# A fixed order of products, sums and splits in the softmax attention of a hybrid block

## The chip, the cores and the metric

One core of a Trainium2 chip. The metric is device time of one execution in microseconds (us). The core has TensorE (PE, with a stream of its own for weight loads, PEld), VectorE (DVE), ScalarE (ACT), GpSimd (POOL) and SyncE (SP), which issues most DMAs. Each of these runs its own queue of instructions strictly in order; semaphores hold an instruction until what it needs on other engines is done. A scheduler arranges the program into these queues when the kernel is built.

## What is computed

Four residual blocks on x of shape (2, 1024, 512), all in fp32: a chunked linear attention, a gated FFN with quantized weights (called f), a softmax attention (b), and the same FFN again (g).

```
x = x + attn_a(layernorm(x))      # 4 heads of 128, chunks of 128 tokens, 2 x 8 chunks
x = x + ffn(layernorm(x))         # 512 -> 1408 -> 512
x = x + attn_b(layernorm(x))      # 512 wide, one head, 2 x 1024 tokens
x = x + ffn(layernorm(x))

# attn_a, per chunk
attn  = (q k^T) * beta * tril(exp(cla - cla^T))    # cla: cumulated log of alpha
y     = attn v + (q state) * exp(cla)
kw    = k * beta * exp(cla_end - cla)              # the weighted keys
state = state * exp(cla_end) + kw^T v

# attn_b
out = softmax(Q K^T / sqrt(512)) V W_o

# ffn
down(silu(gate(x)) * up(x)),  W = (wq - 128) * scale
```

## The kernel before

**Products.** Every large product is made of three: each operand is split into a high half (a copy in a reduced format, on ScalarE) and a low half (the rest, a subtraction on VectorE or GpSimd), and hi·hi, hi·lo and lo·hi are added up in PSUM (`split`, L83; `mm3`, L95). A product in this text is one TensorE instruction of 512 columns. There are 8 PSUM banks, and 12 shared buffers of 128 x 2048 fp32 ("slots"), given out in turn: a new slot waits until its last user has been read.

**Order.** The code emits steps, and the scheduler orders them on each engine by data and its own priorities. `behind(instructions)` (L76) sets an edge: what is emitted inside is put, on the same engine, after those instructions in the queue. It adds no wait on data. DMAs issued from SP and from POOL stand in these engines' queues with the rest.

**Stage A (L338 to L718)** runs over 16 tiles t of 128 tokens. For each: projections `pWk`, `pWv` (24 products, `kv_tile`), norms of the keys (`k_norm`, L543 on: square on ScalarE, sum and factors `s1`, `s2` on VectorE, a power and the weighted keys `kw` on GpSimd), the keys' transpose `pkT` and its copy `kT`, `pd` (kw^T v), the chunk's outputs `pl` and `pg`, and the scores `pS`. `decay(t)` (L494 on) masks `row` on GpSimd (L500) and makes the decays `dec` with four exponentials on ScalarE (L512). Between tiles, `fill[t]` holds steps that prepare later stages: norms of later rows, moves, and `a_split`, which splits the transposed input of later tiles (`xT_a`).

**Layer norms into transposed form** (`ln_norm`, `ln_move`, L175 to L210): a normalised tile is transposed in 32 x 32 blocks by VectorE into a buffer `y` (L195), of which there is one, and 16 DMAs a block of 512 tokens move the pieces to their places in `xT` (L205). A line in `ln_move` chooses the queue that issues them. `combine` (L223 on) then makes the operands of a seven-product scheme: B11, B21, B12, B22 and the sums T1 to T4, each split and in a slot of its own.

**FFN (L721 to L855)** makes two passes of 1024 tokens over 11 hidden blocks of 128. Per block: products P1, P6, P5, P7 into X, Y, Z, V, copies and sums on ScalarE and VectorE (`u2`, `up`), then P2, P3, P4, and the gated result split into `hs`, in part on GpSimd. Each pass ends with eight output tiles (`pof`, `pog`). During it, steps of what comes next are handed out: the argument `after` holds, for FFN f's second pass, norms and moves of attention b's first rows and the 12 steps of their `combine`.

**Attention b (L858 to L1123)** has two batches b of 1024 tokens. Weights are loaded by `blocks` (L860, DMAs L868): `wvo` for the values, `wm` for the queries, both into slots. `v_tile` makes eight value tiles (`pvb`, 12 products each), `q_proj` the queries (`pqb`). Then four cycles n, each for two tiles of 128 query rows: `scores_head` (P1, P6, P5, P7: 24 products into psX, psY, psZ, psV, then the copies and sums `u2b`, `upb`), a `between` (24 products: two query projections or an `out_b`), `scores_tail` (P2, P3, P4: 18 products, then the softmax of both tiles). The scores' left operands A11, S2, S1, S3 (for the head) and A12, A22, S4 (for the tail) come from `q_operands`, each with a cast on ScalarE and a subtraction on VectorE (`opA`, `opS`).

Probabilities go through DRAM: `probs_T` transposes 32 x 32 blocks on VectorE into `py`, writes them by one DMA (L996) and reads them back by four (L1004) into `ptl`, then splits them into `pth` and `ptl`. `out_b(b, i)` (`pob`, 24 products) takes these and the value tiles. `do(steps, n)` hands out n steps of norms, moves or `combine`, behind the last softmax.

Of the kernel before, what the change touches and what calls it, by code (L numbers as in the profile page):

```python
# [34 lines left out]
def hybrid_block_kernel(ctx: ExitStack, tc: tile.TileContext, a, out):  # L35
# [59 lines left out]
    def mm3(ps, lhs_hi, lhs_lo, rhs_hi, rhs_lo, first, last):  # L95
        nc.tensor.matmul(ps, lhs_hi, rhs_hi, start=first, stop=False)  # L96
        nc.tensor.matmul(ps, lhs_hi, rhs_lo, start=False, stop=False)  # L97
        return nc.tensor.matmul(ps, lhs_lo, rhs_hi, start=False, stop=last).ins  # L98

# [97 lines left out]
    def ln_move(nm, st, b):  # L197

        if b == 0:
            lnT[nm, st] = slot(f"xT_{nm}{st}").rearrange("p (k c) -> p k c", k=KD)  # L200
        y = lnY[nm, st]
        xf = lnT[nm, st].bitcast(F32).rearrange("p k (i b q) -> p (k i) b q", i=ST, b=4)
        queue = nc.gpsimd if (nm, st) in (("b", 2), ("b", 3), ("g", 0), ("g", 1)) else nc.sync
        for c in range(4):
            queue.dma_start(  # L205
                out=xf[32 * b : 32 * (b + 1), :, c, :],
                in_=y[32 * c : 32 * (c + 1), b].rearrange("p k i q -> p (k i) q"),
            )
# [129 lines left out]
    with ExitStack() as actx:  # L338
# [201 lines left out]
        def k_norm(t, after=None):  # L540
# [15 lines left out]
            if t % NC < NC - 1:  # L556
                s2 = mp.tile([P, H], F32, tag="s2", name=f"s2{t}")
                nc.vector.tensor_tensor(s2, s1, ec[:, 1, i, :], ALU.mult)
                kw = tl("kw", t)
                weighted = nc.gpsimd.tensor_tensor(kw, kf, s2.unsqueeze(2).to_broadcast([P, H, P]), ALU.mult)  # L560
                normed[t] += (weighted.ins,)
            kva[t] = kf, kw, v
# [118 lines left out]

        fill[3].insert(0, lambda: a_split(2))
        fill[7].insert(0, lambda: a_split(3))
        moving = combine("f", 0)
        wcs, loads = [], []
        for t in range(NT):
# [12 lines left out]
            if t + 1 < NT:  # L699
                decay(t + 1)  # L700
            with behind(normed.get(t + 1, (weighed,))):
# [19 lines left out]
    def ffn(src, dst, nm, wcs, moving, ended, after):  # L721
# [3 lines left out]
        with ExitStack() as fctx:  # L725
# [5 lines left out]
            for pr in range(2):  # L731
# [86 lines left out]
                for i in range(2 * ST):  # L818
# [25 lines left out]
                    if pr == 0 and i == 4:  # L844
                        wcs = [stationary(n, f"{nm}1") for n in range(2)]

    ffn(
        x1,
# [4 lines left out]
        spilled,  # L853
        (ln_steps(x2, "b", 0) + ln_steps(x2, "b", 1), combine("b", 0)),
    )  # L855
# [4 lines left out]
    with ExitStack() as bctx:  # L860
# [57 lines left out]
        def score_product(ps, b, n, nm, first):  # L918
            a_, x = {
                "P1": ("A11", "B11"), "P2": ("A12", "B21"), "P3": ("S4", "B22"), "P4": ("A22", "T4"),  # L920
                "P5": ("S1", "T1"), "P6": ("S2", "T2"), "P7": ("S3", "T3"),
            }[nm]
            o, w = QA[b, n, a_], XT["b", b, x]
            for k in range(2):
                for i, j in ((0, 0), (0, 1), (1, 0)):
                    nc.tensor.matmul(  # L926
                        ps,
                        o[:, i, k],
                        w[:, j, k],
                        start=first and k == 0 and i + j == 0,  # L930
                        stop=k == 1 and i == 1,
                        skip_group_check=nm != "P6",
                    )

        def scores_head(b, n):
# [6 lines left out]
            up = bp.tile([P, 512], F32, tag="up", name=f"upb{b}{n}")  # L942
            nc.scalar.copy(up, Z)
            nc.vector.tensor_tensor(Z, Z, u2, ALU.add)
            nc.vector.tensor_tensor(V, V, u2, ALU.add)
            nc.vector.tensor_tensor(up, V, up, ALU.add)
            heads[b, n] = X, Z, V, up
# [9 lines left out]
        def softmax(t, halves):  # L957
# [3 lines left out]
            nm = mp.tile([P, 1], F32, tag="nm", name=f"nm{t}")  # L961
            nc.vector.tensor_tensor(nm, mx[:, 0:1], mx[:, 1:2], ALU.max)
            nc.vector.tensor_scalar(nm, nm, -SC, None, ALU.mult)
            pe = bp.tile([P, T], F32, tag="pe", name=f"pe{t}")
# [10 lines left out]
        def probs_T(b, i):  # L975
# [4 lines left out]
            if t == NT - 2:  # L980
# [3 lines left out]
                for s in range(2):  # L984
                    ps = psum(f"ppt{t}_{s}").rearrange("p (k c) -> p k c", k=4)
                    ks = slice(s * 4, s * 4 + 4)
                    for k in range(4):
                        n = (s * 4 + k) * P
                        nc.tensor.transpose(ps[:, k, :], pe[:, n : n + P], ident)
                    split(hi[:, ks], lo[:, ks], ps)  # L990
# [12 lines left out]
            for r in range(4):  # L1003
                nc.sync.dma_start(  # L1004
                    out=raw[32 * r : 32 * (r + 1)].rearrange("p k (c q) -> p (k c) q", c=4), in_=placed[r]
                )
            with behind(last):
                for s in range(2):
                    ks = slice(s * 4, s * 4 + 4)
                    split(hi[:, ks], lo[:, ks], raw[:, ks])  # L1010
            ptT[t] = hi, lo, ri

# [23 lines left out]

        qs, QA, heads, pes, ptT, vs, last = {}, {}, {}, {}, {}, {}, []

        def do(steps, n):
            with behind(last):  # L1040
                for _ in range(n):
                    steps.pop(0)()

        def cycle(b, n, between):

            scores_head(b, n)
            if n == 0:
                q_operands(b, 0, True)
            if n < 3 and n != 1:
                q_operands(b, n + 1, False)  # L1050
            between()
            if n == 1:
                q_operands(b, 2, False)
            scores_tail(b, n)
            if n < 3:
                q_operands(b, n + 1, True)

        wvo = blocks(vo_d, "wvo0_")
        wm = blocks(m_d, "wm")
        for b in range(NB):  # L1060
            nm, src, g = ("b", x2, 2) if b == 0 else ("g", x3, 0)
            norm = ln_steps(src, nm, g) + ln_steps(src, nm, g + 1)
            if b == 0:
                for kt in range(NK):
                    v_tile(0, kt)
                do(norm, 4)
                q_proj(0, 0, range(KD))
                q_operands(0, 0, False)
                do(norm, 4)
            else:  # L1070
                do(moving, 1)
                out_b(0, 5)
                q_proj(1, 0, range(KD))
                q_operands(1, 0, False)
                do(moving, 4)
                out_b(0, 6)
                do(norm, 2)
                out_b(0, 7)
                wvo = blocks(vo_d, "wvo1_")
                for kt in (4, 5, 6, 7):  # L1080
                    v_tile(1, kt)
                do(moving, 2)
                for kt in range(4):
                    v_tile(1, kt)
                do(norm, 2)
                do(moving, 4)
                do(norm, 4)
            cycle(b, 0, lambda: q_proj(b, 1, (0, 1)))
            do(norm, 2)
            for i in (0, 1):  # L1090
                probs_T(b, i)
            do(norm, 2)
            cycle(b, 1, lambda: q_proj(b, 1, (2, 3)))
            do(norm, 4)
            for i in (2, 3):
                probs_T(b, i)
            out_b(b, 0)
            if b:
# [3 lines left out]
            for i in (4, 5):  # L1102
                probs_T(b, i)
            out_b(b, 2)
            if b:
# [5 lines left out]
            if b == 0:  # L1111
                for i in (6, 7):
                    probs_T(b, i)
                out_b(b, 4)
        do(moving, 3)
        out_b(1, 4)
        for i in (6, 7):
            probs_T(1, i)
        do(moving, 3)
        out_b(1, 5)  # L1120
        out_b(1, 6)
        wcs = [stationary(n, "g0") for n in range(2)]
        ended = (out_b(1, 7),)  # L1123

# [64 lines left out]
```

## Time and profile before

| | us |
|---|---|
| median of 3 runs | 968.31 (967.44 to 969.77) |
| profiled execution | 972.67 |
| its span | 970.8 |
| TensorE busy in it | 943.2 |
| VectorE busy | 722.3 |
| ScalarE busy | 408.5 |
| GpSimd busy | 213.5 |

The mean TensorE clock granted in the span was 0.989 of full speed. DMAs moved 162 MB, 167 GB/s on average. Matmuls are pipelined: one of 512 columns is listed with 0.39 us, but starts 0.227 us after the one before it. "Idle before" is time in which an engine had nothing to run ahead of an instruction, and the name behind the arrow is what it waited for: `PE pob L96 <- ACT pth L85` reads as TensorE's product for `pob` in line 96 waiting for ScalarE's cast into `pth` in line 85. Line numbers are those of the kernel before.

### The profile page before, as it was taken

How to read it: one execution, taken by the hardware profiler on the slowest of the kernel's cores; microseconds unless marked ns; L12 is line 12 of the kernel's file. 1: busy time of each engine (PE TensorE's matmuls, PEld its weight loads, DVE VectorE, ACT ScalarE, POOL GpSimd, SP SyncE). 2: the span in 40 equal slices, each digit the busy share in tenths (PEclk: the TensorE clock that was granted, in tenths of full speed). 3: DMA queues.
4: the chain of work that ended last, by engine and by line, in shares of the span. 5: the costliest groups of instructions: out<-in, count | busy, mean ns of one | idle time of the engine just before them, and what ended most of it. 6: DMA issues, size and time to landing. Idle time of an engine off the chain costs nothing.

```text
span 970.8 us, 13238 instructions
## 1 busy us (share of the span) xinstructions
PE 943.2 (97%) x4402; PEld 777.9 (80%) x4402; DVE 722.3 (74%) x1473; ACT 408.5 (42%) x791; POOL 213.5 (22%) x310
## 2 busy tenths in 40 slices
PE   8999999999999999999899989999999999999998
PEld 6788787888888888888687767888788878888887
DVE  7766766768999699779626976848876966976654
ACT  4643434344565344344124432434443533534421
POOL 5442413433454011111040140022400221001100
PEclk9999999999999999999899999999999999999999
DMA  9536456664888457623720697615769772464112
GB/s 312 167 101 168 135 126 184 181 183 152 328 316 284 120 184 262 199 44 117 262 74 3 151 194 198 196 23 129 174 163 300 262 202 45 173 230 150 39 56 97
DMA packets 219828, 162.17 MB, mean 167 GB/s; under 512 B 155056, under 2 KB 170736, under 8 KB 219760
## 3 DMA queue, kind: packets, MB, share of 16 engines
q1 hardware_dynamic: 217712, 157.13, 53.5%
q0 software_dynamic: 2048, 4.20, 2.0%
q8 instruction: 35, 0.57, 0.2%
q14 instruction: 33, 0.27, 0.1%
HBM read 104.76 MB, written 41.84 MB: 151 GB/s over the span
## 4 chain that ended last, share of the span: by engine, by line
PE 72%; DVE 10%; DMA 9%; SPq 4%; issue 2%; ACT 2%; POOL 1%; DVEq 0%; POOLq 0%; ACTq 0%
PE pog L833 4%; PE pog L832 4%; PE pXg L328 4%; PE pVg L328 4%; PE pZg L328 4%; PE pVf L328 3%; SPq L205 3%; PE pZf L328 3%; PE pXf L328 3%; PE pob L96 2%; PE pob L98 2%; PE pob L97 2%; PE pYg L328 2%; PE psX L926 2%; PE pvb L96 2%
## 5 line engine op out<-in xcount | busy, mean ns | idle before, releaser
L832 PE MATMUL pog<-wdg,hsg 128*128 128x512 f32 (+1 forms) x165 | 60.3, 375 | 0.0
L833 PE MATMUL pog<-wdg,hsg 128*128 128x512 f32 (+1 forms) x165 | 60.2, 375 | 0.0
L833 PE MATMUL pof<-wdf,hsf 128*128 128x512 f32 x154 | 59.3, 390 | 0.3 <-DVE hsf L86 0.3
L832 PE MATMUL pof<-wdf,hsf 128*128 128x512 f32 x154 | 59.1, 389 | 0.0
L96 PE MATMUL pob<-vh,pth 128*128 128x512 f32 x128 | 50.8, 397 | 6.3 <-ACT pth L85 6.3
L97 PE MATMUL pob<-vl,pth 128*128 128x512 f32 x128 | 50.2, 392 | 0.0
L98 PE MATMUL pob<-vh,ptl 128*128 128x512 f32 x128 | 50.0, 391 | 0.0
L328 PE MATMUL pVg<-T_g,wcg 128*128 128x512 f32 x176 | 47.5, 392 | 1.9 <-DVE upg L794 1.9
L86 POOL TENSOR_TENSOR hsg<-sgg,hsg 128x128 fp32r<-128x128 f32 x40 | 17.7, 463 | 143.2 <-ACT hsg L85 143.2
L328 PE MATMUL pXg<-B_g,wcg 128*128 128x512 f32 x176 | 48.0, 398 | 0.0
L328 PE MATMUL pVf<-T_f,wcf 128*128 128x512 f32 x176 | 46.6, 389 | 0.0
L328 PE MATMUL pXf<-B_f,wcf 128*128 128x512 f32 x176 | 46.0, 391 | 0.2 <-DMA wcf<-wc 0.2
L117 POOL TENSOR_TENSOR rs_b<-ve_b,mhalf 128x1 f32<-128x1 f32 x16 | 12.9, 810 | 144.6 <-DVE ve_b L115 144.5
L328 PEld LDWEIGHTS pVg<-T_g,wcg 128*128 128x128 f32 x176 | 33.0, 188 | 9.1 <-DVE upg L794 2.3
L328 PEld LDWEIGHTS pXg<-B_g,wcg 128*128 128x128 f32 x176 | 34.1, 194 | 7.3
L328 PEld LDWEIGHTS pXf<-B_f,wcf 128*128 128x128 f32 x176 | 32.9, 188 | 7.4 <-DMA wcf<-wc 0.7
L328 PEld LDWEIGHTS pVf<-T_f,wcf 128*128 128x128 f32 x176 | 33.0, 188 | 7.0 <-DVE upf L794 0.2
L832 PEld LDWEIGHTS pog<-wdg,hsg 128*128 128x128 f32 x165 | 31.1, 188 | 5.7
L833 PEld LDWEIGHTS pog<-wdg,hsg 128*128 128x128 f32 x165 | 31.0, 188 | 5.6
L117 POOL TENSOR_TENSOR rs_g<-ve_g,mhalf 128x1 f32<-128x1 f32 x16 | 9.2, 580 | 118.5 <-DVE ve_g L115 118.2
L96 PEld LDWEIGHTS pob<-vh,pth 128*128 128x128 f32 x128 | 24.1, 189 | 13.3 <-ACT pth L85 8.4
L833 PEld LDWEIGHTS pof<-wdf,hsf 128*128 128x128 f32 x154 | 28.9, 188 | 6.8 <-DVE hsf L86 0.8
(332 smaller groups left out, 2749.5 us busy)
## 6 DMA issues: line engine op xcount, KB each, us to landing
wcg<-wc SPq DMA_DIRECT2D x22, 896.0 KB, 6.7
wc<-wcf SPq DMA_DIRECT2D x11, 896.0 KB, 5.3
wcf<-wc SPq DMA_DIRECT2D x11, 896.0 KB, 5.9
p<-py SPq DMA_DIRECT2D x15, 512.0 KB, 3.5
ptl<-p SPq DMA_DIRECT2D x60, 128.0 KB, 3.0
xin_a<-in_x SPq DMA_DIRECT2D x16, 256.0 KB, 4.3
xra<-in_x SPq DMA_DIRECT2D x16, 256.0 KB, 3.3
row<-cl SPq DMA_DIRECT2D x16, 256.0 KB, 4.1
```

The lines of the kernel that those rows point to most:

```text
L86: return c.ins, (eng or nc.vector).tensor_tensor(lo, src, hi.bitcast(F32), ALU.subtract).ins
L96: nc.tensor.matmul(ps, lhs_hi, rhs_hi, start=first, stop=False)
L97: nc.tensor.matmul(ps, lhs_hi, rhs_lo, start=False, stop=False)
L98: return nc.tensor.matmul(ps, lhs_lo, rhs_hi, start=False, stop=last).ins
L117: rsqrt[:] = [nc.gpsimd.tensor_tensor(rs, ve, mhalf, ALU.pow).ins]
L205: queue.dma_start(out=xf[32 * b : 32 * (b + 1), :, c, :], in_=y[32 * c : 32 * (c + 1), b].rearrange("p k i q -> p (k i) q"),)
L328: nc.tensor.matmul(ps, w[:, m, k * P : (k + 1) * P], o[:, s, k, :], start=first and k == 0 and s == 0, stop=k == 1 and s == 1, skip_group_ ...
L832: nc.tensor.matmul(ps, hs[i][0][:, j], wd[j][:, ds], start=j == 0, stop=False)
L833: nc.tensor.matmul(ps, hs[i][1][:, j], wd[j][:, ds], start=False, stop=j == KH - 1)
L926: nc.tensor.matmul(ps, o[:, i, k], w[:, j, k], start=first and k == 0 and i + j == 0, stop=k == 1 and i == 1, skip_group_check=nm != "P6",)
```

## The change

- Stage A: `decay(t+1)` is queued behind the weighted keys of tile t+1, where there are any; filling steps are queued behind `s2` and `kw` too; `a_split` is the last filling step of tiles 2 and 6 rather than the first of tiles 3 and 7.
- FFN f's tail gets six of the 12 steps of attention b's `combine` (B11, B21, B12, B22, the first difference, T1). The other six, with T3, T2 and T4, come after the first four value tiles. Value tiles 4 to 7, which need B12 and B22, go first. The weights `wm` are loaded after these steps. With fewer steps ahead, the loads of `wvo` stand earlier in SP's queue: between the last loads and stores of FFN f's residual rows.
- `ln_move`: attention b's block 2 is issued half by SP and half by GpSimd (before: GpSimd); FFN g's blocks 2 and 3 by GpSimd (before: SP). Blocks b3, g0, g1 stay on GpSimd, the rest on SP.
- Attention b: `array` puts each group of products (value tile, query projection, head, `between`, tail, `out_b`) behind the ends of the group before on TensorE, so that the groups run one after another. `ends` collects these last products in `mm3` and `score_product`.
- `probs_split`, taken out of `probs_T`, splits the probabilities behind the sums of the next cycle's head (`summed`), not behind the last softmax when they were written. `q_operands` is called at other places. The row maximum and its scaling (`nm`) are one VectorE instruction, not two.

```diff
     def mm3(ps, lhs_hi, lhs_lo, rhs_hi, rhs_lo, first, last):
...
-        return nc.tensor.matmul(ps, lhs_lo, rhs_hi, start=False, stop=last).ins
+        end = nc.tensor.matmul(ps, lhs_lo, rhs_hi, start=False, stop=last).ins
+        ends[id(ps)] = end
+        return end
...
-        queue = nc.gpsimd if (nm, st) in (("b", 2), ("b", 3), ("g", 0), ("g", 1)) else nc.sync
         for c in range(4):
-            queue.dma_start(
+            sync = nm in "af" or (nm == "b" and (st < 2 or st == 2 and c % 2))
+            (nc.sync if sync else nc.gpsimd).dma_start(
...
-                nc.vector.tensor_tensor(s2, s1, ec[:, 1, i, :], ALU.mult)
+                scaled = nc.vector.tensor_tensor(s2, s1, ec[:, 1, i, :], ALU.mult).ins
...
-                normed[t] += (weighted.ins,)
+                normed[t] = squared, scaled, weighted.ins
...
-        fill[3].insert(0, lambda: a_split(2))
-        fill[7].insert(0, lambda: a_split(3))
+        fill[2].append(lambda: a_split(2))
+        fill[6].append(lambda: a_split(3))
...
             if t + 1 < NT:
-                decay(t + 1)
+                with behind(normed[t + 1][2:]):
+                    decay(t + 1)
...
-        (ln_steps(x2, "b", 0) + ln_steps(x2, "b", 1), combine("b", 0)),
+        (ln_steps(x2, "b", 0) + ln_steps(x2, "b", 1), of_b[:6]),
...
-            nc.scalar.copy(up, Z)
+            copied = nc.scalar.copy(up, Z).ins
...
-            nc.vector.tensor_tensor(up, V, up, ALU.add)
+            summed[:] = copied, nc.vector.tensor_tensor(up, V, up, ALU.add).ins
...
-            nc.vector.tensor_tensor(nm, mx[:, 0:1], mx[:, 1:2], ALU.max)
-            nc.vector.tensor_scalar(nm, nm, -SC, None, ALU.mult)
+            nc.vector.tensor_scalar(nm, mx[:, 0:1], mx[:, 1:2], -SC, ALU.max, ALU.mult)
...
-            with behind(last):
+            ptT[t] = hi, lo, ri
+
+        def probs_split(b, i, after):
+            hi, lo, _ = ptT[b * NK + i]
+            with behind(after):
                 for s in range(2):
                     ks = slice(s * 4, s * 4 + 4)
-                    split(hi[:, ks], lo[:, ks], raw[:, ks])
-            ptT[t] = hi, lo, ri
+                    split(hi[:, ks], lo[:, ks], lo[:, ks].bitcast(F32))
...
+        def array(fn, *args):
+
+            before = list(ends.values())
+            ends.clear()
+            with behind(before):
+                return fn(*args)
...
         def cycle(b, n, between):
 
-            scores_head(b, n)
-            if n == 0:
-                q_operands(b, 0, True)
-            if n < 3 and n != 1:
-                q_operands(b, n + 1, False)
-            between()
+            array(scores_head, b, n)
+            if n > 0:
+                for i in (2 * n - 2, 2 * n - 1):
+                    probs_split(b, i, summed)
+            if n in (0, 2):
+                with behind(summed):
+                    q_operands(b, n + 1, False)
+            array(between)
             if n == 1:
                 q_operands(b, 2, False)
-            scores_tail(b, n)
+            array(scores_tail, b, n)
             if n < 3:
-                q_operands(b, n + 1, True)
+                with behind(last):
+                    q_operands(b, n + 1, True)
...
-        wm = blocks(m_d, "wm")
+        moving = of_b[6:]
...
             if b == 0:
-                for kt in range(NK):
-                    v_tile(0, kt)
-                do(norm, 4)
-                q_proj(0, 0, range(KD))
-                q_operands(0, 0, False)
-                do(norm, 4)
+                for kt in (4, 5, 6, 7):
+                    array(v_tile, 0, kt)
+                do(moving, 6)
+                wm = blocks(m_d, "wm")
+                do(norm, 8)
+                for kt in range(4):
+                    array(v_tile, 0, kt)
+                array(q_proj, 0, 0, range(KD))
             else:
                 do(moving, 1)
-                out_b(0, 5)
-                q_proj(1, 0, range(KD))
-                q_operands(1, 0, False)
+                array(out_b, 0, 5)
+                array(q_proj, 1, 0, range(KD))
+                for i in (6, 7):
+                    probs_split(0, i, last)
...
+            q_operands(b, 0, False)
+            q_operands(b, 0, True)
```

More of the change, by code (lines that the diff above doesn't have):

```diff
@@ L97, in mm3 @@
         nc.tensor.matmul(ps, lhs_hi, rhs_lo, start=False, stop=False)
-        return nc.tensor.matmul(ps, lhs_lo, rhs_hi, start=False, stop=last).ins
+        end = nc.tensor.matmul(ps, lhs_lo, rhs_hi, start=False, stop=last).ins
+        ends[id(ps)] = end
+        return end
+    ends = {}
     def new_xT(name):
@@ L845, in ffn @@
                         wcs = [stationary(n, f"{nm}1") for n in range(2)]
+    of_b = combine("b", 0)
     ffn(
@@ L925, in score_product @@
                 for i, j in ((0, 0), (0, 1), (1, 0)):
-                    nc.tensor.matmul(
+                    ends[nm] = nc.tensor.matmul(
                         ps,
@@ L932, in score_product @@
                         skip_group_check=nm != "P6",
-                    )
+                    ).ins
         def scores_head(b, n):
@@ L988, in probs_T @@
                         n = (s * 4 + k) * P
-                        nc.tensor.transpose(ps[:, k, :], pe[:, n : n + P], ident)
+                        ends[s] = nc.tensor.transpose(ps[:, k, :], pe[:, n : n + P], ident).ins
                     split(hi[:, ks], lo[:, ks], ps)
@@ L1035, in v_tile @@
             vs[b, kt] = h_, l_
-        qs, QA, heads, pes, ptT, vs, last = {}, {}, {}, {}, {}, {}, []
+        qs, QA, heads, pes, ptT, vs, last, summed = {}, {}, {}, {}, {}, {}, [], []
         def do(steps, n):
@@ L1063, in hybrid_block_kernel @@
             if b == 0:
-                for kt in range(NK):
-                    v_tile(0, kt)
-                do(norm, 4)
-                q_proj(0, 0, range(KD))
-                q_operands(0, 0, False)
-                do(norm, 4)
+                for kt in (4, 5, 6, 7):
[6 more added lines that the diff above has]
+                array(q_proj, 0, 0, range(KD))
             else:
                 do(moving, 1)
-                out_b(0, 5)
-                q_proj(1, 0, range(KD))
-                q_operands(1, 0, False)
+                array(out_b, 0, 5)
+                array(q_proj, 1, 0, range(KD))
+                for i in (6, 7):
+                    probs_split(0, i, last)
                 do(moving, 4)
-                out_b(0, 6)
+                array(out_b, 0, 6)
                 do(norm, 2)
-                out_b(0, 7)
+                array(out_b, 0, 7)
                 wvo = blocks(vo_d, "wvo1_")
                 for kt in (4, 5, 6, 7):
-                    v_tile(1, kt)
+                    array(v_tile, 1, kt)
                 do(moving, 2)
                 for kt in range(4):
-                    v_tile(1, kt)
+                    array(v_tile, 1, kt)
                 do(norm, 2)
@@ L1087, in hybrid_block_kernel @@
                 do(norm, 4)
+            q_operands(b, 0, False)
+            q_operands(b, 0, True)
+            if b == 0:
+                do(norm, 2)
             cycle(b, 0, lambda: q_proj(b, 1, (0, 1)))
-            do(norm, 2)
             for i in (0, 1):
@@ L1093, in hybrid_block_kernel @@
             cycle(b, 1, lambda: q_proj(b, 1, (2, 3)))
-            do(norm, 4)
             for i in (2, 3):
                 probs_T(b, i)
-            out_b(b, 0)
+            do(norm, 4 if b == 0 else 6)
+            array(out_b, b, 0)
             if b:
@@ L1103, in hybrid_block_kernel @@
                 probs_T(b, i)
-            out_b(b, 2)
+            array(out_b, b, 2)
             if b:
@@ L1113, in hybrid_block_kernel @@
                     probs_T(b, i)
[L1114 to L1121, printed above, removed]
+                array(out_b, b, 4)
+        array(out_b, 1, 4)
+        array(probs_T, 1, 6)
+        probs_T(1, 7)
+        probs_split(1, 7, last)
+        do(moving, 6)
+        array(out_b, 1, 5)
+        array(out_b, 1, 6)
         wcs = [stationary(n, "g0") for n in range(2)]
-        ended = (out_b(1, 7),)
+        ended = (array(out_b, 1, 7),)
     out_t = [out[t * P : (t + 1) * P, :] for t in range(NT)]
```

## The prediction

> **What bounds the kernel now.** First the page's busy shares and its rows in 40 slices:
>
> ```profile
> PE 943.2 (97%) x4402; PEld 777.9 (80%) x4402; DVE 722.3 (74%) x1473; ACT 408.5 (42%) x791; POOL 213.5 (22%) x310
> ...
> PE   8999999999999999999899989999999999999998
> ...
> PEclk9999999999999999999899999999999999999999
> ```
>
> TensorE sets the time; nothing else is near it. The change leaves its work alone (each product stands in both kernels), so it can only move TensorE's gaps. Next, for whom PE waited (us in total, times, longest):
>
> ```profile
> PE pob L96 <- ACT pth L85: 6.3, 4, 3.1
> PE pvb L96 <- DMA wvo<-vo: 4.8, 1, 4.8
> PE pd L582 <- POOL kw L560: 3.5, 3, 2.0
> PE pVg L328 <- DVE upg L794: 1.9, 1, 1.9
> PE pab L391 <- DVE xT_a L86: 1.7, 2, 0.9
> ...
> PE psX L926 <- ACT u2b L940: 0.8, 1, 0.8
> ```
>
> Five rows, 18.2 us, each in a place that the diff touches. Then the granted clock in stretches around those places (PE, PEld, DVE, ACT and POOL busy, PEclk, DMA share, GB/s):
>
> ```profile
> 212.00:215.80 3.80, 1.80 (x16) 1.56 (x15) 0.78 (x2) 2.86 (x5) 1.65 (x2) 1.00 0.99 380
> 215.90:219.20 3.30, 3.30 (x17) 3.30 (x17) 2.23 (x6) 1.28 (x2) 2.05 (x2) 0.50 0.30 103
> 471.90:478.60 6.70, 4.26 (x10) 3.39 (x11) 5.37 (x11) 0.00 (x0) 1.48 (x2) 0.50 0.98 371
> ...
> 564.10:567.40 3.30, 2.88 (x7) 2.30 (x8) 2.31 (x6) 0.89 (x2) 3.30 (x6) 0.50 1.00 260
> 697.20:700.50 3.30, 3.30 (x9) 2.57 (x8) 1.55 (x4) 0.59 (x1) 2.80 (x5) 0.50 0.99 197
> 792.80:796.10 3.30, 3.30 (x9) 2.51 (x9) 2.17 (x5) 1.92 (x4) 0.88 (x2) 0.50 0.65 240
> ```
>
> After each wait of 1.85 us or more, PE runs at half clock for 3.4 us (6.8 us, partly idle, after the longest); waits up to 1.3 us show none. So a long wait costs about 3.4/2 = 1.7 us more; after the 4.8 us wait, PE works 478.7 - 474.3 = 4.4 us at half clock, 2.2 us lost. Waits plus clock are what the change can win: 18.2 + 4 x 1.7 + 2.2 = 27.2 us.
>
> The Trainium skill ("TensorE: Matmul & The Clock Gate", section "HAM oscillation — how this bites in real kernels") lets gaps under some 3.4 us pass without a slower clock. The four half-clock stretches after waits of 1.85 to 3.1 us contradict it, and I go by them; by the rule the win would be 4 x 1.7 = 6.8 us smaller.
>
> **Stage A: weighted keys, split of x.** PE's 2.0 us wait is explained by GpSimd's order:
>
> ```profile
> 212.82 0.64 POOL L500 TENSOR_SCALAR_AFFINE_SELECT row<-row 128x512 f32<-128x512 f32 x1 [5.80 <-DVE sWv L536]
> 213.42 1.04 POOL L560 TENSOR_TENSOR kw<-sWk,s 128x512 f32<-128x512 f32 x1
> ...
> 226.07 1.04 POOL L560 TENSOR_TENSOR kw<-sWk,s 128x512 f32<-128x512 f32 x1 [7.09 <-DVE s L558]
> ```
>
> The first `kw` stood behind the mask of a later tile's `row`; the second waited for DVE's `s2` (L558), itself behind filling steps. The change queues the mask and exps of a tile's `decay` behind that tile's `kw`, and filling steps behind `s2` and `kw`. That removes 3.5 us of waiting and one clock penalty of 1.7. What then becomes late is `decay`: four exps of 0.39 us on ACT, now directly ahead of the copy `kT` (0.58). On ACT's order this is a push of 4 x 0.39 = 1.6 us at most; I count nothing, since `decay` still has the projections of a tile (24 products, 5.4 us) before its use, and keep 0 to 1.6 us for one tile where ACT's queue holds two `decay`s. `a_split` starts a tile earlier, so the low halves that PE awaited twice (1.7 us) are there. **6.9 us** (range 4 to 8).
>
> **FFN f to attention.** SP's loads of the values' weights, and PE's first product on them (timeline: start, duration, engine, idle before and its releaser):
>
> ```profile
> 470.64 1.85 SPq L868 DMA_DIRECT2D wvo<-vo  x4
> ...
> 474.34 0.80 PE L96 MATMUL pvb<-wvo,B_b 128*128 128x512 f32 x1 [4.77 <-DMA wvo<-vo]
> ```
>
> The loads were issued after the last T slots came free and landed as PE stood. With only the first six steps of the combination in FFN f's tail, T2 to T4 move behind the first value tiles, and the four `wvo` loads are queued on SP some 15 us earlier, behind the last residual loads. Their landing of 3.7 to 11.2 us (median 6.6) fits there. What moves behind them in SP's queue are four `wm` loads, first needed by `q_proj` eight value tiles later (8 x 12 x 0.227 = 21.8 us). Gain 4.8 + 2.2 = **7.0 us**; if half the landing stays open, 3.5.
>
> The batch's moves of normalised rows into transposed position (L205): half of block 2's go to SP. GpSimd issues one per 0.651 us, SP one per 0.627: 16 take 10.4 us on one queue, 5.2 on two. They start when the last value tile frees their slot and feed nothing before the next batch's combination; DVE's next transposes stand behind them, ahead of the first operands, with `q_proj` (48 products, 10.9 us) as cover: 0, and up to 3 us if they land late.
>
> **Attention: fixed order.** Head (24 products), `between` (24), tail (18) and `out_b` (24) now run strictly one after another on PE; before, the scheduler wove them together and the earliest `out_b` came too soon. Tail 0 ended about 532.5 and `pob` waited until 541.9: 9.4 us for softmax, transpose, round trip through DRAM and cast. For the second pair it was 552.8 to 564.5, 11.7 us, the longest wait. In the new order, tail 0 to `out_b` 0 is 24 + 24 + 18 = 66 products x 0.227 = 15.0 us, and pairs after it have 90 or more (20.4 us). So the four waits, 6.3 us, and the two clock penalties, 3.4, go: 9.7.
>
> Against it: an order that is fixed can't step over a late operand. In a head, Y's operand `S2` comes second, 6 products (1.4 us) in. For heads 0 it is built right after `q_proj`'s last copy: before, 0.8 us idle; after, with all of tile T2's and T4's casts of 1.05 us on the same ACT queue, perhaps 0.5 more each: 1.0 together. For heads 2, `q_operands` stands in ACT's queue behind two `pth` casts (2 x 0.59) that wait for the DRAM round trip, and four exps with their reads (2.9 us). PE can cover that with the tail's rest and `out_b` 0; I can bound the wait only by rows: 0 below, 3.1 above (the longest that PE waited for ACT). I take the middle, 1.5, for two heads: 3.0, without a clock penalty since 1.5 is under 1.85. The splits of the probabilities now wait in line for the head's sums (`summed`), 5.4 us after the tail's end, inside the 15.0. Merging the two tiny `nm` operations saves 0.15 us on the softmax chain, which is hidden. Net 9.7 - 1.0 - 3.0 = **5.7 us** (from 9.7 down to about -4: both heads 2 at 3.1 with clock, 9.6, and heads 0 at 2 each).
>
> **FFN g: moves on GpSimd.** SP's queue and DVE in the timeline:
>
> ```profile
> 777.86 7.62 SPq L205 DMA_DIRECT2D xT_g<-y_g  x8
> ...
> 788.86 0.71 DVE L195 STREAM_TRANSPOSE y_g<-xn_g 128x512 f32<-128x512 f32 x1 [5.46 <-DMA xT_g<-y_g]
> ```
>
> DVE stood 5.5 us at a transpose whose buffer those moves still read; SP had a weight load between the two halves and the second half took 7.6 us. `upg` came late and PE waited 1.9. After: 32 moves go from SP to GpSimd. Sixteen in a row take 10.4 us there (771.8 to 782.2), landed 2.1 later, at 784.3, and the transposes are queued further back on DVE. Behind the moves on GpSimd stand the `hsg` parts of two hidden blocks (0.47 each), up to 6.5 us later than before; ACT and DVE want them some 6 us after that. The second 16 start near 802 and are needed by the next combination near 831. SP's queue, freed, lets weight loads go sooner. Gain 1.9 + 1.7 = **3.6 us**, 0 if the `hsg` parts come late.
>
> The Trainium skill ("DMA: Bandwidth & Descriptors", section "Issuing engine by pattern") sends plain moves to SP as the faster issuer, which speaks against this part. The trace's rows (0.651 against 0.627) make the difference 0.4 us per 16. The page's first-byte times (about 1 against 0.6 us) would delay each batch's landing by an estimated 0.4 us more, and the sum by nothing.
>
> **Sum.** 6.9 + 7.0 + 5.7 + 3.6 = 23.2 us. The profiled execution took 972.67 us (span 970.8 and 1.9 around it), so it would take 949.5; that one lies 4.4 us above the median of 968.31, and taking 23.2 from the median gives **945**.
>
> **The rivals.**
> (a) The heads lose nothing: all 27.2 us are won, **941**. For it: heads 1 and 3 have their operands a block early. Against it: each head of the kernel before that ran without a wait could step to another product; the new one can't.
> (b) The fixed order gives back what it wins in attention: 6.9 + 7.0 + 3.6 = 17.5 stay, **951**. For it: ACT's queue ahead of `S2` is over 4 us long. Against it: 42 products (9.5 us) run between `q_proj` and head 2.
> (c) One part outside attention fails, the largest one being stage A or the weights: 23.2 - 7.0 = 16.2, **952**. For it: slots and queues decide, and the loads must find a free slot early. Against it: the slots they take belong to products already read.
> (d) Slower: `S2` late in all eight heads. Each costs w + 1.7 (clock), against 27.2: from w = 27.2/8 - 1.7 = 1.7 us the change loses; at 3.1, the longest wait for ACT, 8 x 4.8 - 27.2 = 11.2 more than before, **979.5**. For it: the same engine order in every head. Against it: before, only one wait of 0.8 us shows in heads.
> (e) The change doesn't do what it says, since the fixed order binds only each engine's queue and the waits were for data: gaps remain but move, 968 within 0.2%. Against it: the gaps' causes above are queue positions.
>
> **Chances.** Forecast 0.42, (a) 0.17, (b) 0.14, (c) 0.12, (d) 0.10, (e) 0.05. A measurement of this kernel can tell about 0.2% (2 us) from no change. Faster: the forecast and (a) to (c), 0.85; same: (e) less 0.01 for a small loss, 0.04; slower: (d) and that 0.01, 0.11. The range reaches from a little under (a), 936, over (b) and (c), to their sum of losses, where one part fails and attention also gives back its gain: 968.3 - 10.5 = 958, plus 4 us for unlisted waits: 962.
>
> **What would show it.** Right: no row `pvb` on `wvo`, `pob` on `pth`, `pd` on `kw` or `pVg` on `upg` above 0.5 us among PE's waits; half-clock stretches gone at these places; PE's busy share at 98 to 99%. Wrong: a new row `psY` on ACT's `opS` with several us; a half-clock stretch in each attention cycle; DVE or ACT waiting for GpSimd's `hsg` in FFN g; `pS`/`kT` late in stage A.

## The result and the profile after

The changed kernel takes 958.25 us in the median of 6 runs (955.0 to 959.41), the kernel before 969.84 beside it. The ratio is 0.9877, 95% interval 0.9856 to 0.9898: some 12 us faster, half of what was forecast. The profiled execution took 956.25 us, its span is 954.4; the profiles of the two kernels lie 16.4 us apart, which is more than the medians do.

First the page of the changed kernel: busy shares, PE's row in 40 slices, and the granted clock.

```profile
PE 936.0 (98%) x4402; PEld 773.9 (81%) x4402; DVE 727.2 (76%) x1457; ACT 412.3 (43%) x793; POOL 235.0 (25%) x334
...
PE   8999999999999999999999999999999999999998
...
PEclk9999999999999999999999999999999999999999
```

Then for whom PE waits in it (us in total, times, longest):

```profile
PE psY L932 <- ACT opS L85: 2.6, 3, 2.0
PE pYf L332 <- POOL wcf L316: 1.9, 1, 1.9
PE pXf L332 <- DMA wcf<-wc: 1.7, 1, 1.7
PE pS L601 <- ACT kT L576: 1.5, 2, 1.1
...
PE pog L837 <- ACT hsg L85: 1.1, 2, 0.9
PE pd L586 <- POOL kw L564: 0.8, 1, 0.8
PE pog L838 <- DVE hsg L86: 0.7, 1, 0.7
```

The rows for `wvo`, `upg`, `pab` and, all but 0.8 us, `kw` are gone, and so is `pth`. New or larger are `psY` (longest at the first head), `wcf` and `kT` at stage A's end, `pXf` at 368.5 us (weights loaded again for FFN f's second pass, 1.7 us against 0.2 before) and `pog` at FFN g's first outputs.

To set the stages side by side I summed, over each stretch of the trace, how much later than 0.227 us (0.111 us for 128 columns) each product started after the one before it. This is all time that PE lost, waits and slow clock together. "Again" is the same changed kernel profiled a second time, among the experiments below.

| us lost on PE | before | after | after, again |
|---|---|---|---|
| start, 0 to 75 us | 6.4 | 6.8 | 6.9 |
| stage A and the first FFN blocks, 75 to 275 | 11.1 | 9.9 | 10.7 |
| rest of FFN f, 275 to 450 | 2.3 | 3.1 | 2.4 |
| FFN f to attention, 450 to 500 | 7.1 | 0.0 | 0.0 |
| attention, 500 to 725 | 14.7 | 7.0 | 9.4 |
| FFN g, 725 to the end | 4.6 | 3.1 | 3.2 |
| sum | 46.2 | 29.9 | 32.7 |

The weights' part is won in full. In stage A and FFN g the listed waits went and almost as much came back within some 30 us. Three places show how.

**Stage A: the first FFN weights.** GpSimd sums the first weight block's codes; DVE's row of the same time stands under it (timeline: start, duration, engine, idle before and releaser).

```profile
239.01 3.37 POOL L315 TENSOR_TENSOR wcf<-wcf 128x256 fp32r<-128x256 f32 x1 [7.10 <-ACT wcf L299]
242.34 0.72 POOL L317 TENSOR_TENSOR wcf<-wcf 128x256 fp32r<-128x256 f32 x1
...
238.24 2.35 DVE L86 TENSOR_TENSOR T_f<-xT_f,T_f 128x1024 fp32r<-128x1024 f32 x2
240.50 0.69 DVE L86 TENSOR_TENSOR V<-stg_Vl,V 128x512 fp32r<-128x512 f32 x1
241.11 0.69 DVE L86 TENSOR_TENSOR V<-stg_Vr,V 128x512 fp32r<-128x512 f32 x1
241.71 0.69 DVE L621 TENSOR_TENSOR xra<-pl,xra 128x512 f32<-128x512 f32 x1
```

The same kind of sum takes 0.72 us when DVE leaves it alone, and 3.37 here. It starts inside a run of DVE sums with two operands in SBUF and ends at 242.38, 0.6 us after the last of them (241.80). It ended while DVE's next sum, which has an operand in PSUM (`pl`), was running. PE waits 1.9 us for the result.

**Stage A: the copy of the keys.** ACT's queue, and PE's wait behind it:

```profile
222.38 2.46 ACT L516 ACTIVATE dec<-row,ncl 128x128 f32<-128x128 f32 x8 [6.63 <-POOL row L504]
224.73 0.57 ACT L576 COPY kT<-pkT 128x512 f32<-128x512 f32 x1
...
225.35 1.16 PE L601 MATMUL pS<-qT,kT 128*128 128x128 f32 x8 [1.06 <-ACT kT L576]
```

Eight exponentials, those of two tiles, stand in one piece ahead of the copy.

**FFN g's first outputs.** GpSimd's queue, and PE:

```profile
794.07 1.32 POOL L86 TENSOR_TENSOR hsg<-sgg,hsg 128x128 fp32r<-128x128 f32 x2 [5.43 <-ACT hsg L85]
795.34 9.03 POOL L209 DMA_DIRECT2D xT_g<-y_g  x14
804.38 0.96 POOL L86 TENSOR_TENSOR hsg<-sgg,hsg 128x128 fp32r<-128x128 f32 x2
...
813.04 0.50 PE L837 MATMUL pog<-wdg,hsg 128*128 128x512 f32 x1 [0.29 <-ACT hsg L85]
814.40 0.50 PE L837 MATMUL pog<-wdg,hsg 128*128 128x512 f32 x1 [0.86 <-ACT hsg L85]
815.60 0.50 PE L838 MATMUL pog<-wdg,hsg 128*128 128x512 f32 x1 [0.69 <-DVE hsg L86]
```

The `hsg` parts of a late hidden block stand behind 14 moves, so the scheduler put the last products of outputs 0 and 1 behind output 2. These close late, their operand buffers come free late, and the casts for outputs 3 and 4 are late: from 812.4 to 815.6 us, 2.6 us are lost.

### The profile page after: what moved, and what is told of

The parts are those of the page before. It is cut to its first block, busy times and chain, and to the rows that moved or that the text cites. A ratio compares the mean times of both kernels' runs of the same rounds, so it can differ in the third digit from the quotient of the medians.

```text
span 954.4 us, 13226 instructions
## 1 busy us (share of the span) xinstructions
PE 936.0 (98%) x4402; PEld 773.9 (81%) x4402; DVE 727.2 (76%) x1457; ACT 412.3 (43%) x793; POOL 235.0 (25%) x334
## 4 chain that ended last, share of the span: by engine, by line
PE 81%; DVE 6%; DMA 6%; ACT 3%; issue 2%; POOL 1%; SPq 1%; DVEq 0%; POOLq 0%; ACTq 0%
PE pog L838 4%; PE pVg L332 4%; PE pZg L332 4%; PE pXg L332 4%; PE pog L837 4%; PE pZf L332 4%; PE pVf L332 4%; PE pXf L332 3%; PE pof L838 3%; PE pof L837 3%; PE pob L98 3%; PE pob L96 3%; PE pob L97 2%; PE pYg L332 2%; PE pYf L332 2%
## 5 line engine op out<-in xcount | busy, mean ns | idle before, releaser
L209 POOL DMA_DIRECT2D xT_g<-y_g x64 | 41.3, 653 | 35.5 <-DVE T_b L86 28.6
L121 POOL TENSOR_TENSOR rs_g<-ve_g,mhalf 128x1 f32<-128x1 f32 x16 | 12.5, 790 | 138.4 <-DVE ve_g L119 138.3
L332 PE MATMUL pXg<-B_g,wcg 128*128 128x512 f32 x176 | 46.2, 389 | 0.0
```

The costliest lines, as they stand in the source:

```text
L121: rsqrt[:] = [nc.gpsimd.tensor_tensor(rs, ve, mhalf, ALU.pow).ins]
L209: (nc.sync if sync else nc.gpsimd).dma_start(out=xf[32 * b : 32 * (b + 1), :, c, :], in_=y[32 * c : 32 * (c + 1), b].rearrange("p k i q -> ...
L332: nc.tensor.matmul(ps, w[:, m, k * P : (k + 1) * P], o[:, s, k, :], start=first and k == 0 and s == 0, stop=k == 1 and s == 1, skip_group_ ...
```

## The experiments

Ratios are to the kernel before on the same chip, with 95% intervals; the changed kernel's is 0.9877.

**Stage A's order undone.** In the changed kernel:

```diff
-                normed[t] = squared, scaled, weighted.ins
+                normed[t] += (weighted.ins,)
...
-                with behind(normed[t + 1][2:]):
-                    decay(t + 1)
+                decay(t + 1)
...
-        fill[2].append(lambda: a_split(2))
-        fill[6].append(lambda: a_split(3))
+        fill[3].insert(0, lambda: a_split(2))
+        fill[7].insert(0, lambda: a_split(3))
```

> The changed kernel with its stage-A part undone: decay, the filling steps and a_split are ordered as in the kernel before. First theory: the part removed 6 us of waits, but most of it came back in the same stage (kT behind eight exps of decay, the FFN's first weights late on GpSimd), as the two profiles' excess over 50 to 275 us shows (about 11 us before, 10 after): this kernel takes 1 to 3 us more than the changed one, 959 to 961. Rival: the part is worth its predicted 6.9 us and other parts fell short: about 965.

Measured: 955.59 us, 0.9879 (0.9848 to 0.9910), no slower than the changed kernel. PE's waits in it:

```profile
PE pd L586 <- POOL kw L564: 3.2, 2, 1.6
...
PE pab L395 <- DVE xT_a L86: 1.1, 2, 0.7
...
PE pYf L332 <- POOL wcf L316: 0.3, 1, 0.3
```

The waits for `kw` and `xT_a` are back, those for `kT` and nearly all of `wcf` are not. GpSimd's first sum starts at 234.6 us and takes 1.59 us, against 239.0 and 3.37. The part takes about as much as it gives: the first theory's 1 to 3 us more would be a ratio of 0.989 to 0.991, the result lies just under that, and the interval shuts out the rival (6.9 us would be 0.995).

**FFN g's moves on SP again**, blocks 2 and 3:

```diff
-            sync = nm in "af" or (nm == "b" and (st < 2 or st == 2 and c % 2))
+            sync = nm in "af" or (nm == "b" and (st < 2 or st == 2 and c % 2)) or (nm == "g" and st > 1)
```

> The changed kernel with FFN g's blocks 2 and 3 moved by SP as in the kernel before. First theory: on GpSimd the second block's 14 moves stand ahead of the last hsg parts, the first outputs close late and PE waits 2.6 us at the outputs of the pass; on SP this wait goes and the wait for upg (1.9 us, with or without 1.7 us of half clock) returns: between 1 us less and 2 us more than the changed kernel, 957 to 960. Rival: the moves on GpSimd are worth the predicted 3.6 us: about 962.

Measured: 957.32 us, 0.9884 (0.9856 to 0.9912). The wait for `upg` is back with 2.3 us and the rows for `pog` are gone; FFN g loses 3.0 us against 3.1. That is the first theory: one wait was given for another.

**The early weights alone**, in the kernel before: `of_b[:6]` in FFN f's tail, value tiles 4 to 7 first, `do(moving, 6)` and `wm` after them, then value tiles 0 to 3.

> The kernel before with one part of the change: six steps of the combination in FFN f's tail, value tiles 4 to 7 first, the values' weights loaded early, then the other six steps. First theory: the wait of 4.8 us for wvo goes, and with it the 2.2 us of half clock: 6 to 7 us less than before, about 963. Rival: loads hidden but a later wait takes their place (the scheduler's order of the heads, late T2 to T4): under 4 us less, 966 or more.

Measured: 962.15 us, 0.9934 (0.9908 to 0.9959), 6.4 us less by the ratio and 4.7 between the medians (966.88 before). PE loses nothing between 450 and 500 us, and 13.6 in attention (before: 14.7), with the waits for `pth` still 6.7 us. The part stands by itself and is about half of the whole gain.

**Without the fixed order**: `array` only calls its function.

```diff
-            before = list(ends.values())
-            ends.clear()
-            with behind(before):
-                return fn(*args)
+            return fn(*args)
```

> The changed kernel without the fixed order of product groups on PE: array calls its function and nothing else; the splits behind the head's sums and all else stay. First theory: the fixed order alone removes the waits for pth: they return, 6 to 9 us more than the changed kernel, 964 to 967. Rival: the later splits and operand calls do most of it and the order costs waits for S2: the same as the changed kernel within 2 us, or less.

Measured: 956.97 us, 0.9888 (0.9860 to 0.9916). PE waits for `pth` once, 1.3 us, and 2.0 for `opS`. The rival: it isn't the fixed order alone that takes the waits away. But the run tells little of what a woven order costs, since the scheduler by itself now keeps nearly the fixed one: the first `pob` starts 14.6 us after the end of tail 0's last product, as against 15.0 in the changed kernel and 13.5 (0.9 of it waiting) in the kernel before.

**Splits put back early**, behind the last softmax, with PE's order fixed: `probs_split` dissolved into `probs_T` as before.

> The changed kernel with the splits of the probabilities put back behind the last softmax, as in the kernel before; PE's order stays fixed. First theory: the later splits are what took the waits for pth away (without the fixed order they stayed away), so ACT's cast stands ahead of other work again, with PE waiting at pob or at S2: 3 to 6 us slower than the changed kernel, a ratio to before of 0.991 to 0.994. Rival: the fixed order alone covers the round trip (66 products, 15.0 us), so nothing changes: 0.987 to 0.989.

Measured: 959.33 us, 0.9881 (0.9861 to 0.9900), the rival. One wait of 0.9 us for `pth` is left, at the last pair (722 us): behind the tails before it the products on PE do cover the round trip, with the splits early too.

**Both undone**: early splits and no fixed order.

> The changed kernel with both undone: splits behind the last softmax and no fixed order on PE. First theory: each of the two alone suffices, so only without both the waits for pth of the kernel before come back, 6.3 us of them: ratio 0.993 to 0.995, near that of the early weights alone (0.9934). Rival: the attention's gain comes from neither (places of q_operands, moves split over two queues): 0.987 to 0.989.

Measured: 959.71 us, 0.9896 (0.9868 to 0.9924). The ratio lies a little above the rival's range, which the interval holds whole; it shuts out the first theory's. PE's waits:

```profile
PE psY L932 <- ACT opS L85: 4.2, 2, 3.2
...
PE pob L96 <- ACT pth L85: 0.4, 1, 0.4
```

The waits for `pth` did not come back even now, and here too the first `pob` starts 14.6 us after tail 0. Attention loses 10.4 us here, 8.3 without the order, 11.2 with early splits, 7.0 and 9.4 in the two profiles of the changed kernel, 13.6 with the early weights alone. All but the 8.3 and the 7.0 hold one stretch at half clock of 1.7 us. Without it that is 8.7 with both undone and 11.9 with the early weights alone, so most of what attention won comes from what these two left in place.

What the traces show there is a shorter softmax. In the kernel before, DVE put operands, splits and norms between its steps; the two `nm` instructions of one tile stand 3.4 us apart, and the first probabilities of the second pair leave for DRAM 14.8 us after the end of tail 1's last product (541.0):

```profile
548.20 0.14 DVE L962 TENSOR_TENSOR nm<-mx 128x1 f32<-128x1 f32 x1
...
551.56 0.12 DVE L963 TENSOR_SCALAR nm<-nm 128x1 f32<-128x1 f32 x1
```

```profile
555.77 0.37 SPq L996 DMA_DIRECT2D p<-py  x1
```

This length is 6.2 us in the changed kernel, 7.0 with both undone and 14.6 with the early weights alone. Whether the one `nm` instruction shortens it, or the new places of `q_operands`, or the order in which steps are handed out, no run tells.

**S2 first, block 3 of FFN g on SP.** S2 gets its own buffer and the head's other operands are queued behind its split; `ln_move` sends ("g", 3) through SP. In this kernel S4 is made from A11 and not from S2, so it computes other scores, with as many operations.

```diff
-            nc.vector.tensor_tensor(A["A11"], s1, A["A11"], ALU.subtract)
-            part("S2", A["A11"])
-            part("S1", s1)
-            part("S3", A["A21"])
+            s2 = b1.tile([P, 2, P], F32, tag="s2_", name=f"s2_{b}{n}")
+            nc.vector.tensor_tensor(s2, s1, A["A11"], ALU.subtract)
+            second[:] = part("S2", s2)
+            with behind(second):
+                part("S1", s1)
...
+                part("S3", A["A21"])
```

> The changed kernel with two mends: in q_operands S2 is made first, in a buffer of its own, and the rest is queued behind its split; FFN g's block 3 is moved by SP, block 2 stays on GpSimd. First theory: the waits of psY for opS (2.6 us in the changed kernel) shrink below 1, and those of pog for hsg (1.8 us, with what PE loses around them 2.6) go: 3 to 4 us less than the changed kernel, ratio 0.984. Rival: PE waits at the next operand instead (S1 or S3, now behind S2) and DVE's late transposes make upg late again: 0.987 to 0.988.

Measured: 960.69 us, 0.9893 (0.9870 to 0.9915). `psY` waits 1.0 us and FFN g's outputs not at all, as expected, but two others took their place:

```profile
PE pob L96 <- ACT pth L85: 4.3, 2, 3.8
...
PE pob L98 <- DVE ptl L86: 2.9, 1, 2.9
```

The first of them comes from SP's queue (timeline):

```profile
711.60 1.33 SPq L321 DMA_DIRECT2D wcg<-wc  x3
717.81 5.52 SPq L1011 DMA_DIRECT2D ptl<-p  x4
```

Three weight loads of 896 KB each now stand ahead of the last read of probabilities, whose four issues take 5.5 us, against 2.9 in the changed kernel, where the loads come after them. Neither theory had this. The second wait, for `ptl`, stands in the three kernels that make S2 first and in no other.

**The first codes' sums on DVE**, for block 0 of FFN f's first pass:

```diff
-            nc.gpsimd.tensor_tensor(s1, f(a21), f(a22), ALU.add)
+            eng = nc.vector if j == 0 else nc.gpsimd
+            eng.tensor_tensor(s1, f(a21), f(a22), ALU.add)
```

and the three after it alike.

> The changed kernel with the sums of the first weight block of each FFN pass made from codes computed by DVE, not GpSimd (only the very first block of FFN f lies at stage A's end). First theory: GpSimd's first sum took 3.37 us and ended 0.6 us after DVE's run of four sums of two SBUF operands, 0.7 us being its own length: GpSimd is held by DVE there. On DVE itself the four sums take 4 x 0.42, and PE's wait pYf for wcf (1.9 us) falls under 0.7: 1 to 3 us less than the changed kernel, ratio 0.985 to 0.987. Rival: the wait comes from the late cast on ACT or the load of the codes, and moving the sums leaves it or lengthens it: 0.988 or more.

Measured: 957.46 us, 0.9859 (0.9839 to 0.9879). The sums take 0.42 us each on DVE, and the wait at 241 us is gone; 20 us later PE waits 1.5 us for ACT's next codes. Stage A loses 8.4 us against 9.9 and 10.7. The place is settled; in the time alone it can't be told from the changed kernel.

**The changed kernel again.**

> The changed kernel once more, beside kernels built on it. First theory: its waits stand in the same places (kT and wcf at stage A's end, psY at the first head, pog at FFN g's first outputs), but which of them draws a half-clock stretch differs from the first profile, since the same wait of 2.3 us at the first head drew one in two kernels of five and none in three; ratio 0.986 to 0.990. Rival: the stretches stand where the first profile had them (after wcf alone).

Measured: 957.81 us, 0.9871 (0.9847 to 0.9895). The first theory: the waits stand in the same places and the stretches elsewhere. Stretches by the clock (columns as in the prediction), first of the first profile, then of this one:

```profile
241.63:245.04 3.41, 1.49 (x7) 1.04 (x6) 1.89 (x6) 3.14 (x5) 3.33 (x5) 1.00 0.43 120
245.10:248.40 3.30, 3.30 (x9) 2.60 (x8) 2.36 (x4) 1.81 (x4) 3.30 (x6) 0.50 0.91 341
501.05:504.46 3.41, 2.67 (x12) 1.85 (x10) 1.47 (x5) 2.07 (x6) 0.00 (x0) 1.00 0.00 0
504.46:507.87 3.41, 2.19 (x10) 1.80 (x10) 2.16 (x7) 1.18 (x5) 0.00 (x0) 1.00 0.00 0
505.70:509.00 3.30, 3.30 (x14) 2.72 (x15) 0.92 (x3) 1.30 (x3) 0.00 (x0) 1.00 0.00 0
```

```profile
240.10:243.52 3.42, 1.79 (x8) 1.13 (x6) 3.38 (x8) 1.92 (x4) 3.42 (x3) 1.00 0.56 198
502.96:506.37 3.41, 1.46 (x7) 0.88 (x6) 3.20 (x9) 2.69 (x8) 0.00 (x0) 1.00 0.00 0
506.40:509.70 3.30, 3.30 (x9) 2.60 (x8) 0.42 (x1) 0.58 (x3) 0.00 (x0) 0.50 0.00 0
```

The wait at the first head, 1.96 us in both, is followed by full clock in the first profile and by half clock in the second. At `wcf` it is the other way round: 1.9 us of idle before `pYf` drew a half-clock stretch in the first, and two waits of 2.0 and 2.5 us drew none in the second.

Laid side by side, the stretches show what decides. Within each profile that has several, they start at whole multiples of 3.413 us from one another (in the kernel before: 75, 102, 141 and 169 of them after the first). The lines of 3.41 and 3.42 us above are windows on this grid. In the 14 profiles, without each kernel's start and end, 24 windows at full clock are followed by a half-clock one. In 21 of these PE was idle for 1.85 us or more; in none of some 3,800 others was it idle for more than 1.77. The three exceptions, 1.5 to 1.6 us, lie at FFN g's first outputs, where single products stand apart. So what counts of a wait is the part within one window. At the first head the grid cuts the first profile's wait into 0.73 and 1.22 us, and the second profile's falls into one window. At `wcf` the first profile's 1.9 us fall into one window, and of the second profile's waits at most 1.7 us do.

**Old order in stage A, mended.** The changed kernel with `decay` and the filling steps as before, `a_split` early, ("g", 3) on SP.

> The changed kernel with stage A's decay and filling steps ordered as in the kernel before (a_split stays early), and FFN g's block 3 moved by SP. First theory: stage A is no worse than in the changed kernel, since the waits for kw return but those for kT and wcf go, and the waits of pog at FFN g's outputs (2.6 us with what PE loses around them) go: 2 to 4 us less than the changed kernel, ratio 0.983 to 0.986. Rival: the new order in stage A is worth its price and the block on SP brings the wait for upg back: 0.988 or more.

Measured: 954.17 us, 0.9838 (0.9815 to 0.9861). FFN g loses 0.4 us (3.1 before the mend); stage A loses 10.0 us, the waits for `kw` 4.7. Those for `kT` and `wcf` are smaller, 1.0 us each, but not gone. The time is as the first theory had it.

**All mends.** The changed kernel with S2 first (S4 from S2), the first codes on DVE, ("g", 3) on SP, and

```diff
-                with behind(normed[t + 1][2:]):
+                with behind((*normed[t + 1][2:], copied)):
                     decay(t + 1)
...
-        wcs = [stationary(n, "g0") for n in range(2)]
+        with behind(read):
+            wcs = [stationary(n, "g0") for n in range(2)]
```

where `copied` is `kT`'s copy and `read` the last issued read of probabilities.

> The changed kernel with five mends: block 3 of FFN g moved by SP; the first weight block's sums on DVE; decay queued behind kT's copy too; S2 first in q_operands, with S4 made from it; FFN g's first weight loads behind the last read of probabilities. First theory: the waits for pog (2.6 us), wcf (1.9), kT (1.1) and most of psY (2.6) go, some 6 us, and the loads no longer delay the last probabilities: ratio 0.980 to 0.983. Rival: DVE, with more to do at stage A's end, is late with something else there, and only the 2.6 us of pog stay won: 0.985 to 0.987.

Measured: 952.01 us (951.34 to 954.78), 0.9825 (0.9802 to 0.9848). It lies in the first theory's range and has the lowest median of all, 5.8 us below the changed kernel on the same chip; from the kernel just above, 2.2 us, the intervals don't tell it apart. Some of PE's waits:

```profile
PE pob L98 <- DVE ptl L86: 2.9, 1, 2.9
...
PE pXf L333 <- ACT wcf L299: 1.0, 1, 1.0
...
PE psY L935 <- ACT opS L85: 1.0, 1, 1.0
...
PE pS L602 <- ACT kT L577: 0.4, 1, 0.4
```

One large wait is left, and DVE's queue shows why: the split of the probabilities stands behind those of FFN g's operands.

```profile
705.57 1.22 DVE L86 TENSOR_TENSOR T_g<-xT_g,T_g 128x1024 fp32r<-128x1024 f32 x1
...
707.37 1.21 DVE L86 TENSOR_TENSOR B_g<-xT_g,B_g 128x1024 fp32r<-128x1024 f32 x1
708.50 1.28 DVE L86 TENSOR_TENSOR ptl<-ptl,pth 128x512 fp32r<-128x512 f32 x2
```

**Old order in stage A, with the mends that are left** (S2 first, the loads behind the read, ("g", 3) on SP, `a_split` early):

> As the kernel with all mends, but with stage A's decay and filling steps ordered as in the kernel before and the sums on GpSimd. First theory: the waits for kw are back (about 3 us), those for kT and wcf are not there: the same as the kernel with all mends or up to 2 us more, 0.981 to 0.985. Rival: stage A in the new order with its mends is clearly better: 3 us more than that kernel, 0.985 or more.

Measured: 953.26 us, 0.9831 (0.9810 to 0.9852): with its new order mended and with its old one, stage A can't be told apart in the time. The waits for `kw` are back with 3.6 us; against the expectation, those for `kT` (1.6) and `wcf` (1.2) stand here too.

## Why only half of the forecast gain came

**What bounds the kernel** was read rightly: only PE's lost time moved, and the time moved with it.

**The clock: the step that failed first.** The prediction put 4 x 1.7 + 2.2 = 9.0 us of its 27.2 on half-clock stretches after waits of 1.85 us or more, from one profile in which all five such waits drew one. That profile had a mean clock of 0.989 and lay 4.4 us above the median; the sum was taken off the median all the same. 35 other runs of the kernel had 0.9933 in the mean, so they lose some 0.004 x 968 = 4 us less to the clock. The 12 runs of the changed kernel had 0.9975. The clock's part of the gain is then about (0.9975 - 0.9933) x 960 = 4.0 us, not 9.0. A wait of about 2 us draws such a stretch only where it falls into one window. With 1.8 us as the limit that is (3.41 + 2.0 - 2 x 1.8) / 3.41 = 0.53 of all positions, an estimate; at the first head it was four profiles of seven. The Trainium skill ("TensorE: Matmul & The Clock Gate", section "Part 1: The HAM clock gate (the "warmup" mystery)") describes the gate as watching windows of 3.4 us that run freely, whatever the kernel does; the grid of 3.413 us in these traces agrees with it. The prediction took from this page only the limit for gaps.

**Stage A: 5.2 us without the clock; measured, 1.2 less in one profile and 1.3 more in the other** (11.1 less 1.7, against 9.9 less 1.7, and 10.7), and nothing in the time when the order was undone. "That removes 3.5 us of waiting" held but for 0.8. "I count nothing" for `decay` failed: the push of up to 1.6 us that it kept for a tile with two `decay`s came, as 1.5 us of waits for `kT`. And the step looked at what is queued behind `kw` on GpSimd, not at what the filling steps feed. Held behind `s2` and `kw`, they run later on DVE; the first FFN codes' load, which waits for one of DVE's `V` splits, is issued at 232.7 us against 228.3 with the old order; the sums of these codes start 4.4 us later on GpSimd, and there they meet more of DVE's sums.

**The weights: 4.8 us, measured 4.9** (7.1 less 2.2 of clock). With the clock 7.0 were forecast, and the part alone gave 4.7 to 6.4.

**Attention: 6.3 less 4.0 without the clock, measured 3.6 to 4.3** (14.7 less two stretches of 1.7, against 7.0, and 9.4 less one). That is more than the forecast 2.3, and for another reason than given. The cover of 15.0 us is there, but the round trips it was held against were read from the wrong rows. 532.5 and 552.8 us are where the last products of later heads end (P7, `opS`); the tails' own last products (P4, `opA`) end at 528.4 and 541.0:

```profile
526.87 1.56 PE L926 MATMUL psV<-T_b,opA 128*128 128x512 f32 x6
...
531.05 1.64 PE L926 MATMUL psV<-T_b,opS 128*128 128x512 f32 x6
...
539.41 1.56 PE L926 MATMUL psV<-T_b,opA 128*128 128x512 f32 x6
541.89 0.50 PE L96 MATMUL pob<-vh,pth 128*128 128x512 f32 x1 [0.91 <-ACT pth L85]
```

So it was 13.5 and 23.6 us, not 9.4 and 11.7. The longest wait stood behind a late softmax on DVE, which no part of the argument looked at, beyond 0.15 us for the merged `nm`, "hidden". The fixed order isn't what the waits hung on. The price was put in the wrong place too. Heads 2 wait 0.4 to 1.1 us in the two profiles, not 1.5; the first head of all waits 2.0, since casts for the tail and S1 stand ahead of S2 in ACT's and DVE's queues.

**FFN g: 1.9 without the clock, measured 0.** The wait for `upg` went as predicted. "The second 16 start near 802 and are needed by the next combination near 831" asked only when the moves must be done, not what stands behind them on GpSimd: the `hsg` parts. The prediction had named them for the first 16 moves; its low case, "0 if the `hsg` parts come late", is what came.

**Sum.** Waits 14.2 and clock 9.0 were forecast. PE's lost time less its clock stretches went from 46.2 - 9.0 = 37.2 to 28.2 and 31.0 us in the two profiles, 6.2 to 9.0 less; with 4.0 of clock this is 10.2 to 13.0, around the 11.6 between the medians. Of the rivals, (c), one part outside attention fails, is nearest in kind: two failed, and the clock with them.

## What to carry to other kernels

Before a wait is struck off, look at what the moved work feeds next on every engine: here nearly all that stage A and FFN g gave was taken back within some 30 us by an engine that now did its work later. When one engine is 97% busy, count only waits that no other wait stands close behind, and take a clock's share from several runs' mean clock rather than from one profile. Before a product is said to wait for a round trip, make sure from the operand's name where that trip begins. A queue that is given more DMAs delays every small operation behind them, also those of the second batch.

## What the runs showed of the hardware

GpSimd's sum of two SBUF operands (0.72 us) took 3.37 us while DVE ran four sums with two SBUF operands each, and `kw` took 1.36 and 1.87 us instead of 1.04 beside such sums. The Trainium skill ("GPSIMD Engine Reference", section "1. Specifications") lists this contention for VectorE instructions with two SBUF inputs; the rows agree, and give its size here: the sum ended only 0.6 us after the whole unbroken run, and on DVE itself, in another run, such sums took 0.42 us. It goes both ways: beside the `kw` that took 1.36 us, one of DVE's `V` splits took 1.53 us instead of 0.69. Waits of 1.95 us at the same place (`psY` at the first head) were followed by half clock in four of the seven profiles that had this wait, and by full clock in three. In the four the whole wait lay in one window of the 3.413 us grid. In the three, at most 1.2, 1.4 and 1.8 us of it did.
